# Graph attention weights as a product of two exponentials, in place of start-up transfers in order of use

## The chip, the cores and the metric

The kernel runs on one core of one Trainium2 chip. The metric is the device time of one launch in microseconds. Before the change the median of three runs is 2511.33 us (2510.76 to 2514.62). The profiled execution has a span of 2509.0 us and a mean granted TensorE clock of 0.994.

## The reference, cut to what matters

128 graphs of 64 nodes with 256 features go through four layers, each followed by a residual sum and a layer norm: a gated graph network (five recurrent steps with message weights), a two-layer perceptron with an RMS norm on aggregated features, a hyperbolic map, and graph attention. All is float32. The change touches the last layer and the start. The last layer is:

```python
h = hidden @ W_w.T + W_b                  # hidden: (128, 64, 256)
a1, a2 = a_w[:256], a_w[256:]
e, f = h @ a1, h @ a2                     # one number per node each
logits = e[:, :, None] + f[:, None, :] + a_b[0]
u = mask * exp(logits)                    # mask: the adjacency, (128, 64, 64), 0 or 1
a = u / sum(u, axis=2, keepdims=True)
h_prime = a @ h
x = layernorm(x + h_prime)
```

## The kernel before

Two graphs are put side by side on 128 partitions, with zeros in the off-diagonal quarters of the 128 x 128 adjacency block. Four such blocks (eight graphs) are a group, and there are 16 groups. Up to four neighbouring groups are in work at once: every operation of every group is recorded with its engine, an assumed duration and what it reads and writes, and a planner that runs when the kernel is built merges the groups into one order of instructions for each engine. So a changed operation or assumed duration changes the whole order.

The assumed durations and the model of transfers in the planner (cut):

```python
def op(self, eng, us, run, w=(), r=(), kb=0): ...       # kb: size of a transfer
# in the planner: a transfer has a bus with a speed, and at most eight are under way
DMA = (2.0, 330.0, 1.0)
TRANSFERS = 8
elif o.kb and e != "POOL":
    t = max(t, self.lands[0])
```

The start (cut): weights are loaded raw, turned on TensorE, and multiplied with each other, so that five steps have their own gate weights. Sixteen transposes of the identity into a bank that nobody reads stand ahead of the first useful ones.

```python
for s in range(NF):
    nc.vector.memset(edge[s].tile(), 0.0)
load(0)                                                  # x and adjacency of group 0, SP queue
# ... small vectors on the POOL queue ...
raw_in(w_hh, "ACT", "h", 0, 4)
raw_in(w_ih, "ACT", "A", 0, 4)
raw_in(w_ih, "ACT", "B", 1, 2)
warm = const.tile([P, NB], F32, name="warm")
flow.op("ACT", 1.5, lambda: nc.scalar.activation(warm, one4, AF.Tanh))
ps_x = bank("ps_x")
for i in range(16):
    pe(128, lambda i=i: nc.tensor.transpose(ps_x[...], ident.tile(), ident.tile()), [ps_x], [ident])
raw_in(w_hh, "SP", "h", 1, 2)
wm_in(0)
load(1)
for l in range(1, L):
    wm_in(l)
raw_in(att_w, "SP", "adjT", 0, 2)
# ... later, also on SP: w1s, w2s (1 MB each)
```

The attention of a group (cut). `wattT` holds the turned weights and three more columns: zeros, and the weights times `a1` and `a2`; `wb_r` holds the bias with a one and two numbers more. So one product gives `h`, a column of ones, `e` and `f`:

```python
ho = u("h", "ho", (P, NB, D + 3))
for b in range(NB):
    ps = bank("ps_a")
    for k in range(KD):
        pe(256, ... matmul(ps[:, :D + 3], x3T[:, k, b*P:(b+1)*P], wattT[:, k, :], k, KD), ...)
    dve(256, ... nc.vector.tensor_add(ho[:, b, :], ps[:, :D + 3], wb_r.tile()), ...)
ps_e = bank("ps_e")
for b in range(NB):
    turn(... nc.tensor.transpose(ps_e[:, b*P:(b+1)*P], ho[:, b, D+1:D+2].to_broadcast([P, P]), ident.tile()), ...)
lg = u("U", "lg", (P, NB, N))
for t in range(2):
    dve(256, ... nc.vector.tensor_tensor(lg[q], tiles_of(ps_e.tile())[q, :, q], ho[q, :, D+2] broadcast, OP.add), ...)
act(256, ... nc.scalar.activation(lg.tile(), lg.tile(), AF.Exp, bias=ab_c.tile()), ...)
for t in range(2):
    dve(256, ... nc.vector.tensor_mul(ed[q, :, q], lg[q], adjT[q, :, q]), ...)
for b in range(NB):
    ps = bank("ps_att")
    pe(257, ... matmul(ps[:, :D + 1], ed[:, b, :], ho[:, b, :D + 1], 0, 1), ...)
    dve(4, ... nc.vector.reciprocal(rd[:, b:b+1], ps[:, D:D+1]), ...)
    dve(256, ... scalar_tensor_tensor(y3[:, b, :], ps[:, :D], rd[:, b:b+1], x3[:, b, :], OP.mult, OP.add), ...)
```

Of the kernel before, what the change touches and what calls it, by code (L numbers as in the profile page):

```python
# [42 lines left out]
class Op:  # L43
    __slots__ = ("eng", "us", "run", "stream", "n", "kb", "need", "then", "bufs", "opens", "id", "way")

    def __init__(self, eng, us, run, stream, n, kb):
        self.eng, self.us, self.run, self.stream, self.n, self.kb = eng, us, run, stream, n, kb
        self.need, self.then, self.bufs, self.opens, self.id, self.way = 0, [], (), None, 0, 0.0


class Plan:


    def __init__(self, flow):
        self.flow = flow
        ops = [o for s in flow.streams for o in s]
        self.need = [o.need for o in ops]
        self.at = [0.0] * len(ops)
        self.uses = {}
        self.clock = dict.fromkeys(flow.AHEAD, 0.75)  # L60
        self.queues = [{e: deque(o for o in s if o.eng == e) for e in self.clock} for s in flow.streams]
        self.banks = [0.0] * BANKS
        self.left, self.first, self.bus, self.done = len(ops), 0, 0.0, 0.0
        self.lands = [0.0] * flow.TRANSFERS
        self.past, self.order = None, []

    def copy(self):
        c = Plan.__new__(Plan)
        c.flow, c.need, c.at, c.uses = self.flow, self.need.copy(), self.at.copy(), self.uses.copy()
        c.clock, c.banks, c.lands = self.clock.copy(), self.banks.copy(), self.lands.copy()  # L70
        c.queues = [{e: d.copy() for e, d in q.items()} if self.first <= s < self.first + 2 * self.flow.WINDOW else q
                    for s, q in enumerate(self.queues)]
        c.left, c.first, c.bus, c.done = self.left, self.first, self.bus, self.done
        c.past, c.order = (self.past, self.order), []
        return c

    def advance(self, until, rank):
# [3 lines left out]
        while self.left and clock["PE"] < until:  # L81
            best = None
            for s in range(self.first, min(self.first + flow.WINDOW, len(self.queues))):
                for e, q in self.queues[s].items():
                    opened = False
                    for _, o in zip(range(flow.AHEAD[e]), q):
                        t = max(clock[e], at[o.id])
                        if o.opens is not None:
                            if opened or not banks or need[o.id]:
                                opened = True  # L90
                                continue
                            t = max(t, banks[0])
                        elif need[o.id]:
                            continue
                        elif o.kb and e != "POOL":
                            t = max(t, self.lands[0])
# [20 lines left out]
            if o.kb:  # L117
                self.bus = max(self.bus, end + flow.DMA[0]) + o.kb / flow.DMA[1]
                end = self.bus + flow.DMA[2]
                if o.eng != "POOL":  # L120
                    self.lands = [*self.lands[1:], end]
# [19 lines left out]
class Flow:  # L141
# [13 lines left out]


    DMA = (2.0, 330.0, 1.0)
    TRANSFERS = 8
# [9 lines left out]
    def op(self, eng, us, run, w=(), r=(), kb=0):  # L168
        o = Op(eng, us, run, len(self.streams) - 1, len(self.ops), kb)
# [46 lines left out]
    def issue(self):  # L216
        self.ways()
        ranks = (lambda s, o: (s, o.n), lambda s, o: (s if o.kb else -s, o.n), lambda s, o: (self.LAG * s - o.way, s, o.n))
# [21 lines left out]
def kernel(  # L240
# [73 lines left out]
    def pe(n, run, w, r):  # L314
        flow.op("PE", {512: 0.86, 256: 0.435, 257: 0.44, 128: 0.23}.get(n, 0.3), run, w, r)
# [31 lines left out]
    def load(g):  # L347
        s = g % NF
        xt = unit("B", s, f"x_{g}", (P, NB, D))
        flow.op("SP", 0.5, lambda: nc.sync.dma_start(xt.tile(), x_rows[g]), [xt], kb=512)  # L350
        for t in range(2):
            q = quads[t]
            flow.op("SP", 0.75, lambda q=q, t=t: nc.sync.dma_start(edge[s][q, :, q], adj_blocks[g, t]),
                    [(edge[s], t)], kb=64)
        loads[g] = xt
# [3 lines left out]
    for s in range(NF):  # L359
        nc.vector.memset(edge[s].tile(), 0.0)  # L360
# [32 lines left out]
    wattT = fixed([P, KD, D + 3], "wattT")  # L393
# [9 lines left out]
    for v, n in ((b_ih, NV), (b_hh, NV), (b1, KH), (rms_w, KH)):  # L403
        flow.op("POOL", 0.55, lambda v=v, n=n, at=at: nc.gpsimd.dma_start(
            vecs[at:at + n, :], v.rearrange("(c p) -> c p", p=P)), [(vecs, at)], kb=3)
        at += n
    flow.op("POOL", 0.55, lambda: nc.gpsimd.dma_start(nmr.tile(), nodemask.rearrange("(k t) n -> k (t n)", t=2)),
            [nmr], kb=32)

# [4 lines left out]

    def raw_in(src, eng, tag, i, n):
        q = {"SP": nc.sync, "ACT": nc.scalar}[eng]
        raw = unit(tag, S, f"raw_{src.tensor.name}{i}", (P, n, D), bufs(tag))
        flow.op(eng, 0.6, lambda: q.dma_start(
            raw.tile(), src.rearrange("(c p) d -> p c d", p=P)[:, 4 * i:4 * i + n, :]), [raw], kb=128 * n)
        raw_of[src.tensor.name, i] = raw  # L420

    wms = []

    def wm_in(l):
        wm = unit("UVZRU"[l], S - l // 4, f"wm{l}", (P, KD, D))
        flow.op("SP", 0.6, lambda: nc.sync.dma_start(
            wm.tile(), w_msg[l].rearrange("(k p) e -> p k e", p=P)), [wm], kb=256)
        wms.append(wm)

    raw_in(w_hh, "ACT", "h", 0, 4)  # L430
    raw_in(w_ih, "ACT", "A", 0, 4)
    raw_in(w_ih, "ACT", "B", 1, 2)

    warm = const.tile([P, NB], F32, name="warm")
    flow.op("ACT", 1.5, lambda: nc.scalar.activation(warm, one4, AF.Tanh))
    ps_x = bank("ps_x")
    for i in range(16):
        pe(128, lambda i=i: nc.tensor.transpose(ps_x[:, i % 4 * P:(i % 4 + 1) * P], ident.tile(), ident.tile()), [ps_x], [ident])
    raw_in(w_hh, "SP", "h", 1, 2)
    wm_in(0)  # L440
    load(1)
    for l in range(1, L):
        wm_in(l)
    raw_in(att_w, "SP", "adjT", 0, 2)
# [43 lines left out]
    for l in range(L):  # L488
# [25 lines left out]
        sums("DVE", 0.7) if l == 0 else sums("POOL", 1.32)  # L514

    w1s = fixed([P, KD, H], "w1s")
    flow.op("SP", 0.6, lambda: nc.sync.dma_start(w1s.tile(), w1.rearrange("(k p) h -> p k h", p=P)), [w1s], kb=1024)
    w2s = fixed([P, KH, D], "w2s")
    flow.op("SP", 0.6, lambda: nc.sync.dma_start(w2s.tile(), w2.rearrange("(k p) d -> p k d", p=P)), [w2s], kb=1024)
# [3 lines left out]
    def everywhere(v, n, name, more=0):  # L523
        t = fixed([P, n + more], name)
        flow.op("POOL", 0.55, lambda: nc.gpsimd.dma_start(
            t[:, :n], bass.AP(tensor=v.tensor, offset=v.offset, ap=[[0, P], [1, n]])), [t], kb=n / 2)
        return t
# [3 lines left out]
    wb_r = everywhere(att_b, D, "wb_r", 3)  # L531
# [17 lines left out]
    pool(0.11, lambda: nc.gpsimd.memset(wattT[:, :, D:D + 1], 0.0), [(wattT, D)])  # L549
    pool(0.11, lambda: nc.gpsimd.memset(wb_r[:, D:D + 1], 1.0), [wb_r])  # L550
    for i in range(2):
        for o, k in ((wattT[:, 0, :], 0), (wattT[:, 1, :], 1), (wb_r.tile(), None)):
            src = wb_r if k is None else (wattT, k)
            dve(256, lambda o=o, i=i: nc.vector.scalar_tensor_tensor(
                junk_d.tile(), o[:, :D], 1.0, a_r[:, i * D:(i + 1) * D], OP.mult, OP.mult,
                accum_out=o[:, D + 1 + i:D + 2 + i]), [src if k is None else (wattT, (k, i))], [src, a_r])

    def group(g):
# [217 lines left out]
        flow.op("SP", 0.5, lambda: nc.sync.dma_start(xr.tile(), x_rows[g]), [xr], kb=512)  # L776
# [145 lines left out]
        ho = u("h", "ho", (P, NB, D + 3))  # L922
        for b in range(NB):
            ps = bank("ps_a")
            for k in range(KD):
                pe(256, lambda ps=ps, b=b, k=k: matmul(
                    ps[:, :D + 3], x3T[:, k, b * P:(b + 1) * P], wattT[:, k, :], k, KD), [ps], [(x3T, b // 2), wattT])
            dve(256, lambda ps=ps, b=b: nc.vector.tensor_add(ho[:, b, :], ps[:, :D + 3], wb_r.tile()),  # L928
                [(ho, b)], [ps, wb_r])
        ps_e = bank("ps_e")  # L930
        for b in range(NB):
            turn(lambda b=b: nc.tensor.transpose(
                ps_e[:, b * P:(b + 1) * P], ho[:, b, D + 1:D + 2].to_broadcast([P, P]), ident.tile()), [ps_e], [(ho, b)])
        lg = u("U", "lg", (P, NB, N))
        for t in range(2):
            q = quads[t]
            dve(256, lambda q=q: nc.vector.tensor_tensor(
                lg[q], tiles_of(ps_e.tile())[q, :, q], ho[q, :, D + 2].unsqueeze(2).to_broadcast([N, NB, N]), OP.add),
                [(lg, t)], [ps_e, ho])
        act(256, lambda: nc.scalar.activation(lg.tile(), lg.tile(), AF.Exp, bias=ab_c.tile()), [lg], [lg, ab_c])  # L940

        for t in range(2):
            q = quads[t]
            dve(256, lambda q=q: nc.vector.tensor_mul(ed[q, :, q], lg[q], adjT[q, :, q]), [(ed, t)], [lg, adjT])
        y3 = rows("y", "y3")
        rd = tiny("rd")
        for b in range(NB):
            ps = bank("ps_att")
            pe(257, lambda ps=ps, b=b: matmul(ps[:, :D + 1], ed[:, b, :], ho[:, b, :D + 1], 0, 1),
               [ps], [ed, (ho, b)])  # L950
            dve(4, lambda ps=ps, b=b: nc.vector.reciprocal(rd[:, b:b + 1], ps[:, D:D + 1]), [(rd, b)], [ps])
# [42 lines left out]
```

## Time and profile before

| what | value |
|---|---|
| time, median of 3 | 2511.33 us |
| span of the profile | 2509.0 us |
| TensorE (PE) busy | 2438.9 us, 97% |
| VectorE (DVE) busy | 1659.8 us, 66% |
| ScalarE (ACT) busy | 1188.6 us, 47% |
| GpSimd (POOL) busy | 179.1 us, 7% |
| moved by the queues | 35.12 MB, mean 14 GB/s |

Busy time of an engine is time in which it had an instruction under way. For each group of instructions the profile gives the number, the busy time, the mean duration in ns, and the idle time of the engine just before, with the instruction that ended it. PE runs the matmuls, PEld loads their weights beside them. A float32 matmul stands as two records; a transpose stands as one. SPq, ACTq and POOLq are the queues from which transfers are issued.

### The profile page before, as it was taken

How to read it: one execution, taken by the hardware profiler on the slowest of the kernel's cores; microseconds unless marked ns; L12 is line 12 of the kernel's file. 1: busy time of each engine (PE TensorE's matmuls, PEld its weight loads, DVE VectorE, ACT ScalarE, POOL GpSimd, SP SyncE). 2: the span in 40 equal slices, each digit the busy share in tenths (PEclk: the TensorE clock that was granted, in tenths of full speed). 3: DMA queues.
4: the chain of work that ended last, by engine and by line, in shares of the span. 5: the costliest groups of instructions: out<-in, count | busy, mean ns of one | idle time of the engine just before them, and what ended most of it. 6: DMA issues, size and time to landing. Idle time of an engine off the chain costs nothing. (4 is left out here: it accounts for less than half of the span.)

```text
span 2509.0 us, 31864 instructions
## 1 busy us (share of the span) xinstructions
PE 2438.9 (97%) x11986; PEld 2047.4 (82%) x11986; DVE 1659.8 (66%) x3725; ACT 1188.6 (47%) x2500; POOL 179.1 (7%) x146
## 2 busy tenths in 40 slices
PE   8999999999999999999999999999999999999995
PEld 6887887888787887887878878887888887878874
DVE  2656677667577676666776766676766665666766
ACT  3444445445445445445454454455445445444643
POOL 4001000000001000000010000010000000000011
PEclk9999999999999999999999999999999999999998
DMA  4000000000000000000000000000000000000000
GB/s 125 1 1 9 1 9 20 1 9 28 1 20 9 20 9 20 1 19 9 1 28 1 20 9 1 9 28 1 20 28 1 11 18 1 9 20 9 1 9 26
DMA packets 39146, 35.12 MB, mean 14 GB/s; under 512 B 9892, under 2 KB 38592, under 8 KB 38992
## 3 DMA queue, kind: packets, MB, share of 16 engines
q1 hardware_dynamic: 37264, 31.20, 3.9%
q8 instruction: 95, 1.56, 0.3%
q10 hardware_dynamic: 1328, 1.31, 0.2%
q0 software_dynamic: 400, 0.57, 0.1%
q14 instruction: 59, 0.48, 0.1%
HBM read 24.69 MB, written 8.39 MB: 13 GB/s over the span
## 5 line engine op out<-in xcount | busy, mean ns | idle before, releaser
L609 PE MATMUL p_hn<-hT,w_hn 128*128 128x256 f32 x1280 | 320.7, 380 | 0.0
L609 PE MATMUL p_in<-agg,w_in 128*128 128x256 f32 x1280 | 311.9, 379 | 0.0
L609 PEld LDWEIGHTS p_in<-agg,w_in 128*128 128x128 f32 x1280 | 241.3, 190 | 32.6 <-issue 1.0
L609 PEld LDWEIGHTS p_hn<-hT,w_hn 128*128 128x128 f32 x1280 | 229.0, 191 | 29.4 <-issue 4.8
L312 PE MATMUL ps_o<-w2s,hid 128*128 128x256 f32 x1024 | 234.0, 381 | 3.4 <-DVE n L905 3.0
L312 PE MATMUL ps_hid<-aggm,w1s 128*128 128x512 f32 x512 | 229.0, 592 | 0.0
L312 PEld LDWEIGHTS ps_o<-w2s,hid 128*128 128x128 f32 x1024 | 193.2, 191 | 30.2 <-issue 3.2
L624 POOL TENSOR_TENSOR rstd<-ve,pow 128x4 f32<-128x4 f32 (+1 forms) x64 | 77.5, 1211 | 1823.6 <-DVE ve L622 1823.5
L713 ACT ACTIVATE V<-V,half_b 128x256 f32<-128x256 f32 x160 | 72.8, 500 | 267.9 <-DVE V L709 267.9
L312 PEld LDWEIGHTS ps_hid<-aggm,w1s 128*128 128x128 f32 x512 | 95.3, 190 | 97.1 <-issue 92.4
L609 PE MATMUL p_r<-hT,a 128*128 128x256 f32 x640 | 155.1, 380 | 7.2 <-ACT U L739 5.9
L609 PE MATMUL p_u<-tA,s 128*128 128x256 f32 x640 | 157.3, 384 | 4.9 <-DVE tA L692 2.3
L609 PE MATMUL p_w<-tA,s 128*128 128x256 f32 x640 | 160.2, 380 | 1.7 <-DVE tA L692 1.7
L609 PE MATMUL p_r<-agg,a 128*128 128x256 f32 x640 | 153.4, 380 | 5.9 <-ACT agg L602 4.9
L609 PE MATMUL p_v<-tB,s 128*128 128x256 f32 x640 | 156.7, 379 | 0.0
L678 ACT ACTIVATE hnb<-p_hn,half_b 128x256 f32<-128x256 f32 x320 | 135.5, 471 | 44.6 <-PE p_hn L609 42.4
L609 PE MATMUL p_v<-tB,na 128*128 128x256 f32 x640 | 153.8, 380 | 2.1 <-DVE V L709 2.0
L722 DVE SCALAR_TENSOR_TENSOR R<-R,hnb 128x512 f32<-128x512 f32 x80 | 56.1, 701 | 150.1 <-ACT R L713 150.0
L609 PE MATMUL p_w<-hT,s 128*128 128x256 f32 x640 | 155.4, 379 | 0.0
L602 ACT COPY agg<-ps_agg 128x512 f32<-128x512 f32 x160 | 93.0, 583 | 119.2 <-PE ps_agg L312 94.4
L312 PEld LDWEIGHTS ps_agg<-edge,hr 128*128 128x128 f32 x1024 | 134.6, 191 | 11.3 <-ACT hr L672 4.9
L609 PEld LDWEIGHTS p_r<-hT,a 128*128 128x128 f32 x640 | 120.2, 190 | 28.4 <-ACT U L739 7.9
(206 smaller groups left out, 4447.1 us busy)
## 6 DMA issues: line engine op xcount, KB each, us to landing
x<-in_x_dram SPq DMA_DIRECT2D x16, 512.0 KB, 3.8
xr<-in_x_dram SPq DMA_DIRECT2D x16, 512.0 KB, 3.5
out_dram<-x_n SPq DMA_DIRECT2D x16, 512.0 KB, 2.8
edge<-in_adj_dram SPq DMA_DIRECT2D x32, 64.0 KB, 2.3
wm<-in_L_gnn_weight_dram SPq DMA_DIRECT2D x5, 256.0 KB, 7.3
w1s<-in_L_gnn_W_dram SPq DMA_DIRECT2D x1, 1024.0 KB, 6.8
w2s<-in_L_gnn_W_dram SPq DMA_DIRECT2D x1, 1024.0 KB, 9.6
aw_in_L_gnn_w_hh_dram<-in_L_gnn_w_hh_dram ACTq DMA_DIRECT2D x1, 512.0 KB, 5.3
```

Of the source, the lines that this page charges most:

```text
L312: nc.tensor.matmul(o, lhsT, rhs, start=(k == 0), stop=(k == nk - 1))
L602: act(512, lambda: nc.scalar.copy(dst[:, :, half(n)], blocks_of(ps.tile())), [(dst, n)], [ps])
L609: pe(256, lambda c=c, k=k: nc.tensor.matmul(ps[:, c * HR:(c + 1) * HR], w[:, k, c * P:(c + 1) * P], v(k), start=first and c == k == 0, sto ...
L624: pool(1.1, lambda: nc.gpsimd.tensor_tensor(rstd[:, :m, :], ve[:, :m, :], pow2[:, :m, :], OP.pow), [rstd], [ve])
L678: act(300, lambda c=c: nc.scalar.activation(hnb[:, c, half(n)], p_hn[:, c * HR:(c + 1) * HR], AF.Identity, bias=half_b[:, 2 * KD + c:2 * K ...
L713: act(256, lambda c=c: nc.scalar.activation(o[:, c, :], src(c), AF.Tanh, bias=half_b[:, i * KD + c:i * KD + c + 1], scale=0.5), [(o, c)], ...
L722: dve(512, lambda: nc.vector.scalar_tensor_tensor(t.tile(), t.tile(), 1.0, hnb[:, :, half(n)], OP.add, OP.mult), [t], [t, (hnb, (n, 0)), ( ...
```

## The change

The weight exp(e_i + f_j + a_b) is exp(e_i) times exp(f_j) with the constant shared out. A factor of the row falls out of the quotient (the code still multiplies it in ahead of the reciprocal and out again behind it, in two small products a block). So the sums can use the plain transposed adjacency with features that are scaled by exp(f_j), and no 64 x 64 matrix of weights is made. The bias of the features is added at the end, since the weights of a row sum to one; with it go the reads and writes of the `edge` tile in this layer. What ScalarE does on the way out of PSUM is an exponential of two columns and a copy with that scale.

At the same time the ordering of the start is left out: the planner's model of transfers, the ordered issue, the warming transposes and the early table load are gone, ten transfers are issued from the ACT queue at once, and the three `edge` tiles are zeroed on POOL instead of DVE.

```diff
-    nc.vector.memset(edge[s].tile(), 0.0)
+    flow.op("POOL", 0.5, lambda t=edge[s]: nc.gpsimd.memset(t.tile(), 0.0), [edge[s]])
 ...
-                        elif o.kb and e != "POOL":
-                            t = max(t, self.lands[0])
-        ranks = (..., lambda s, o: (s if o.kb else -s, o.n), ...)
+        ranks = (..., lambda s, o: (-s, o.n), ...)
-        flow.op("SP", 0.5, lambda: nc.sync.dma_start(xt.tile(), x_rows[g]), [xt], kb=512)
+        flow.op("SP", 4.0, lambda: nc.sync.dma_start(xt.tile(), x_rows[g]), [xt])
 ...
-    raw_in(w_hh, "ACT", "h", 0, 4)
-    raw_in(w_ih, "ACT", "A", 0, 4)
-    raw_in(w_ih, "ACT", "B", 1, 2)
-    flow.op("ACT", 1.5, lambda: nc.scalar.activation(warm, one4, AF.Tanh))
-    for i in range(16):  ... transposes of the identity ...
-    raw_in(w_hh, "SP", "h", 1, 2); wm_in(0); load(1); wm_in(1..4); raw_in(att_w, "SP", "adjT", 0, 2)
+    for src, eng, tags in ((w_hh, "SP", ("h", "h")), (w_ih, "ACT", ("A", "B")), (att_w, "ACT", ("adjT",))):
+        ... one transfer for each tag ...
+    for l in range(L):  ... wm on "ACT" ...
+    ... w1s, w2s on "ACT"; load(1) only after the gate weights ...
 ...
+    dve(256, lambda: nc.vector.tensor_add(a_sum.tile(), a_r[:, :D], a_r[:, D:]), [a_sum], [a_r])
+    dot(... cs, wb_r, a_sum ...); cs = (cs + ab_c) / 2
 ... the attention of a group:
-            dve(256, ... nc.vector.tensor_add(ho[:, b, :], ps[:, :D + 3], wb_r.tile()), ...)
-        ps_e, its four transposes, lg (two additions), one Exp of 128 x 256, two products into ed
+            act(4, ... nc.scalar.activation(hw[:, b, D:], ps[:, D:D + 2], AF.Exp, bias=cs.tile()), ...)
+            act(256, ... nc.scalar.activation(hw[:, b, :D], ps[:, :D], AF.Identity, scale=hw[:, b, D:D+1]), ...)
+        dve(1030, ... nc.vector.tensor_add(x3.tile(), x3.tile(), over(wb_r.tile(), NB)), ...)
         for b in range(NB):
-            pe(257, ... matmul(ps[:, :D + 1], ed[:, b, :], ho[:, b, :D + 1], 0, 1), ...)
-            dve(4, ... reciprocal(rd, ps[:, D:D + 1]))
+            pe(256, ... matmul(ps[:, :D + 1], adjT[:, b, :], hw[:, b, :D + 1], 0, 1), ...)
+            dve(4, ... tensor_mul(rd, ps[:, D:D + 1], hw[:, b, D + 1:]))
+            dve(4, ... reciprocal(rd, rd))
+            dve(4, ... tensor_mul(rd, rd, hw[:, b, D + 1:]))
```

## The prediction

> **What bounds the kernel now.** I read the head of the page first, for the engine that has no time left.
>
> ```profile
> span 2509.0 us, 31864 instructions
> PE 2438.9 (97%) x11986; PEld 2047.4 (82%) x11986; DVE 1659.8 (66%) x3725; ACT 1188.6 (47%) x2500; POOL 179.1 (7%) x146
> ...
> PE   8999999999999999999999999999999999999995
> ```
>
> PE is busy in 2438.9 of 2509 us; only its first and its last slices are not full. So a change brings time in four ways only: work taken off PE, PE idle time at the start, in the middle, or at the end. The table of 50 us windows shared out the 70 us of idle time: 7 us in the first 50, about 31 us in the 47 windows between 50 and 2400, never more than 3.7 in one, and the rest, about 32 us, behind 2400. DVE with 66% and ACT with 47% have slack in the middle; what they do matters there only as latency.
>
> The waits of PE, cut to the first 60 us and then to the time behind 2400 us, show what ends the idle time at both ends (total, times, longest):
>
> ```profile
> PE ps_agg L312 <- DVE edge L655: 3.2, 1, 3.2
> PE ps_x L438 <- POOL ident masks.py:199: 2.5, 1, 2.5
> PE ps_wmT L492 <- DMA wm<-in_L_gnn_weight_dram: 1.4, 1, 1.4
> ```
>
> ```profile
> PE ps_T L579 <- DVE x_n L638: 9.7, 1, 9.7
> PE ps_o L312 <- DVE n L905: 3.0, 1, 3.0
> PE ps_e L932 <- DVE ho L928: 2.7, 5, 1.3
> PE ps_att L312 <- DVE edge L944: 2.4, 1, 2.4
> ```
>
> At the end it is DVE, with the chain of the last two groups, and two of the four lines belong to the attention that is changed. Last, the groups of instructions of the old attention, with shapes kept apart (busy us, mean ns):
>
> ```profile
> L928 DVE TENSOR_TENSOR ho<-ps_a,wb_r 128x259 f32<-128x259 f32 x64 | 26.3, 419 | 15.5 <-PE ps_a L312 15.5
> L932 PE MATMUL ps_e<-ident,ho 128*128 128x128 f32 x64 | 14.1, 279 | 3.3 <-DVE ho L928 3.3
> L937 DVE TENSOR_TENSOR lg<-ps_e,ho 64x256 f32<-64x256 f32 x32 | 13.5, 421 | 11.2 <-PE ps_e L932 11.0
> L944 DVE TENSOR_TENSOR edge<-lg,adjT 64x256 f32<-64x256 f32 x32 | 13.4, 417 | 5.5 <-ACT lg L940 5.0
> L940 ACT ACTIVATE lg<-lg,ab_c 128x256 f32<-128x256 f32 x16 | 8.1, 504 | 21.6 <-DVE lg L937 21.5
> ```
>
> The whole old attention apart from its large products is 53 us of DVE, 8 us of ACT and 64 transposes in 2509 us. What is changed is small.
>
> **What the Trainium skill says.** "TensorE: Matmul & The Clock Gate", section "What's actually happening": PE starts at half its clock and is let to the full one only after some 3.4 us of activity; a pause as long throttles it again. The trace agrees: at 16.75 us, behind a pause of 3.2 us, eight records of the aggregation took 2.04 us; at 22.95 us eight of the same took 1.05. "ScalarE: Activation LUTs", section "Table sets: the hidden batching unit": exp and tanh are in one set, so an exponential among tanhs needs no switch. The trace agrees: of the 33 table loads, 1283 ns each, one stands at the line of the Exp, and the changed program has 33 loads too. Same page, "What ACT_TABLE_LOAD costs": a pointer operand adds about 93 ns to an activation. No row here isolates it; I use it for one estimate below. "DMA: Bandwidth & Descriptors", "Queues, rings and completion order": the DMA engines take packets from the queues in turn, so a queue filled early takes bandwidth from one with urgent data. In the first 20 us the trace has the 16 engines 0.95 busy at 296 GB/s, so there is something to take.
>
> **The change part by part.**
>
> *PE work.* The built program has 6492 PE operations where there were 6572: 64 transposes of `ps_e` and 16 warming ones less. A mean of 279 ns is latency; in a row, transposes start every 0.112 us (at 8.41 us nine loads of transposes took 1.01 us). 64 x 0.112 = 7.2 us off the bound engine. One column less of 259 in 128 products is under half a per cent of the 63.6 us of `ps_a`: 0.2 us. The warming ones ran while PE had nothing to do: nothing. Sum: -7.2 us.
>
> *DVE.* Off: 26.3 + 13.5 + 13.4 = 53.2 us. On: one addition of 128x1024 a group. Additions take 0.419 us at 256 (L928) and 0.684 at 512, so 1.035 ns an element; at 1024 that is 0.684 + 512 x 0.001035 = 1.21 us, times 16 = 19.4. And two small products a block of about 0.16 us like the other small DVE rows: 128 x 0.16 = 20.5. Net -13 us of 1660, in slack.
>
> *ACT.* Off: 8.1 us. On, in each of 64 blocks: an Exp of two columns, 0.207 us like the 128x4 Tanh of the map, plus 0.093 for its pointer, 0.30 (an estimate), and an Identity of 256 columns from PSUM, 0.471 like the `hnb` row. 64 x 0.77 = 49, net +41 us, to 1230 us or 49%. In slack as well; a block takes ACT 0.77 us while PE needs 4 records of 0.215, 0.86 us, for the next one. So ACT keeps up.
>
> *Start.* In the trace, PE stood until 16.75 us for an `edge` product on DVE, which had waited in DVE's order behind a bias product for `a_r` (DVE sat idle 4.9 us until 14.59, "DMA a_r"). The new order has the same trap: a sum of the halves of `a_r` stands as DVE's 14th row, ahead of the transposed-adjacency copy, the `edge` products and the weight copies. And `a_r` is issued later, since POOL first zeroes three `edge` tiles. A POOL memset of 128 columns took 0.20 us and one of 1 column 0.10, so about 0.5 for 512, times three = 1.5 us. From 6.89 to 8.4 us, landing 7.7 us after as before, 16.1; then 0.42 for the sum, 0.68 for the copy, 0.60 for the two products: PE goes on at about 17.9, 1.2 us later. What PE has done by then differs more. Before, 42 transposes (x, both weights, adjacency, first message weight, vectors) were behind it; in the new order only 14 stand ahead of the aggregation. 28 x 0.112 = 3.1 us are still to do. Sum +4.3. The order in which the rest of the start stands then keeps PE fed: all five sets of weight products, 5 x 5.2 us, before the first group.
>
> *End.* The old chain from the last `ps_a` (done about 2494.6) to the first `ps_att` (2497.81) is ho, ps_e, lg twice, exp, edge twice: 3.2 us. The new one is 0.30 + 0.47 and two hand-overs, about 1.0: -2.2. Behind it, three small DVE operations instead of one a block: 4 x 2 x 0.16 = +1.3. The addition of the bias to x3 lies beside the 5.3 us of `ps_a`. The group before it saves about 3.4 us of DVE work on that stretch and gets back 2.5: -0.9. In the old order the third-last group's attention stood in the middle of the last two groups' chains (its `ho` delays the norm at 2422 us, its sums at 2440 to 2444); in the new order it stands some 60 rows of PE earlier, while group 15 still fills PE. That was about 2 us on the chain of the end. Sum: -4 us.
>
> *Middle.* The orders are planned anew with other durations, so 31 us of small gaps are drawn again. I see no reason for a sign: 0, with plus or minus 10.
>
> -7.2 + 4.3 - 4 + 0 = -6.9: 2511.3 - 6.9 = about 2504 us.
>
> **The rivals.** *ACT latency takes the place of DVE latency.* Scale and exponential stand in ACT's order behind whatever came before, and `ps_a` banks are held by two activations instead of one addition. The list of waits has PE waiting for ACT 17 us in all between 60 and 2400 (`U`, `agg`, `x3T`, `hr`, `Z`), more than for DVE in each single line; 41 us more ACT work could raise this. If each of the 16 groups loses 1 us, PE's gain is gone twice over: 2520. Against it: ACT is idle half of the time, and PE has other groups' work to take. *The start is worse than I reckon.* 2 MB of perceptron weights go out on ACT's queue at once beside the x and weights that PE needs; if `a_r` or the message weights land 10 us later, the start costs 15 instead of 4: 2515. Against it: all that the start needs from SP's queue is its first 1.4 MB, and both queues together need 20 us at 296 GB/s for everything. *The new plan is simply better*, with the edge tile free after layer 1 and a shorter chain in every group: if half of the gaps in the middle go, 2490. Against it: hardly any of those gaps are waits of the attention (`ps_e` 0.6 us in the middle).
>
> **Range and chances.** The parts' uncertainty is about 2 us for PE's work, 5 for the start, 5 for the end and 10 for the middle, together some 12. I choose 2504 and 2488 to 2521. Two per cent are 50 us, four times that spread, and only a new systematic stall of 3 us a group would reach it: 0.015 faster, 0.965 the same, 0.02 slower.
>
> **What would show it.** PE busy about 7 us lower, near 2432. In PE's waits up to 60 us, `ps_agg` waits for DVE's `edge` until about 18 us and DVE for `a_r`. DVE near 1647, ACT near 1230, 33 table loads. In the end, no line for `ps_e`, PE's idle time behind the same work 4 us less. I am wrong if PE's waits for ACT in the middle double, if PE is idle over 20 us in the first 60, or if PE busy doesn't fall.

## The result and the profile after

| | before | after |
|---|---|---|
| time, median of 4 runs | 2512.97 us (2510.76 to 2514.8) | 2523.07 us (2522.06 to 2524.53) |
| span of the profile | 2509.0 us | 2522.8 us |
| PE busy | 2438.9 us | 2433.8 us |
| PE idle, 0 to 50 us | 7.0 us | 15.5 us |
| PE idle, 50 to 2400 us | 30.9 us | 40.6 us |
| PE idle behind 2400 us | 32.1 us | 33.0 us |

The ratio after to before is 1.0041, 95% interval 1.0024 to 1.0058: the changed kernel takes some 10 us more, where 7 us less were predicted. First the head of the page of the changed kernel:

```profile
span 2522.8 us, 31907 instructions
PE 2433.8 (96%) x11906; PEld 2039.3 (81%) x11906; DVE 1642.8 (65%) x3738; ACT 1229.5 (49%) x2611; POOL 177.8 (7%) x147
...
PE   7999999999999999999999999999999999999995
```

PE still bounds the kernel and has less to do; DVE and ACT fell and rose as they should. So the 13.8 us of span were lost in PE's idle time. The table of windows says where. Its columns are the stretch, its length, busy us and instructions of PE, PEld, DVE, ACT and POOL, granted clock, share of the DMA engines, GB/s. First the kernel before:

```profile
0.00:50.00 50.00, 42.95 (x197) 33.46 (x198) 13.67 (x43) 15.84 (x38) 15.82 (x26) 0.93 0.47 146
50.00:2400.00 2350.00, 2319.11 (x11471) 1956.18 (x11470) 1569.41 (x3420) 1131.43 (x2382) 148.52 (x109) 1.00 0.03 11
2400.00:2509.00 109.00, 76.87 (x320) 57.80 (x319) 76.75 (x263) 41.36 (x81) 14.77 (x12) 0.91 0.06 20
```

And the changed kernel:

```profile
0.00:50.00 50.00, 34.53 (x143) 25.10 (x144) 11.31 (x34) 12.82 (x32) 19.46 (x29) 1.00 0.48 146
50.00:2400.00 2350.00, 2309.42 (x11389) 1944.17 (x11389) 1548.94 (x3445) 1162.54 (x2467) 144.69 (x108) 1.00 0.04 11
2400.00:2522.80 122.80, 89.84 (x378) 70.01 (x376) 82.55 (x261) 54.13 (x113) 13.68 (x11) 0.87 0.04 13
```

Length minus PE busy is the idle time of the table above: 8.4 us more at the start, 9.7 more in the middle, 0.8 more behind 2400. One correction belongs to it: the 16 warming transposes of the kernel before counted as 3.67 us of busy PE (from 2.47 us on) and are gone. So of the 5.1 us that PE busy fell, 3.7 were never work and 1.4 are left, and the start's loss of idle time, with the warming counted as idle, is 15.5 - (7.0 + 3.7) = 4.8 us.

**The start.** The waits of PE in the first 60 us (total, times, longest):

```profile
PE ps_cols L417 <- DMA vecs<-in_L_gnn_rms_weight_dram: 10.7, 1, 10.7
PE ps_agg L300 <- DVE edge L632: 4.7, 1, 4.7
```

PE did nothing for 10.7 us: its first instruction turns a small vector that the POOL queue brought last, and the instructions behind it stay behind it in PE's order, though the x that eight of them turn had landed at 6.01 us. The timeline of the start (start, us, engine, operation, the idle time before it and who ended it):

```profile
9.26 0.55 POOL L496 DMA_DIRECT2D a_r<-in_L_gnn_a_w_dram  x1 [2.16 <-DMA vecs<-in_L_gnn_b_ih_dram]
10.75 0.28 PE L417 MATMUL ps_cols<-ident,vecs 28*128 28x28 f32 x1 [10.75 <-DMA vecs<-in_L_gnn_rms_weight_dram]
...
17.19 0.42 DVE L531 TENSOR_TENSOR a_sum<-a_r 128x256 f32<-128x256 f32 x1 [5.34 <-DMA a_r<-in_L_gnn_a_w_dram]
...
18.14 0.60 DVE L632 TENSOR_SCALAR edge<-edge 64x256 f32<-64x256 f32 x2
18.79 1.22 PE L300 MATMUL ps_agg<-edge,x 128*128 128x128 f32 x4 [4.72 <-DVE edge L632]
...
20.44 1.91 PE L438 MATMUL ps_w<-ident,w_in_L_gnn_w_hh_dram 128*128 128x128 f32 x8
```

The second wait is the trap of the prediction, link by link: `a_r` issued at 9.26, its sum on DVE at 17.19, the `edge` product behind it, PE at 18.79. It is the one that counts. Only 14 instructions stand between the two waits, and the aggregation behind them would have stood until 18.79 if they had been done earlier; so on this reading the first wait cost nothing of its own, though no run takes it away alone.

The last line shows half speed. Behind the two pauses eight transposes take 1.91 us, where eight of the same kind took 1.04 us at 7.64 us of the kernel before. This is what the Trainium skill describes in "TensorE: Matmul & The Clock Gate", section "What's actually happening": behind a pause PE starts at half its clock. The trace agrees with that, though the half speed lasted about 5 us of work (18.79 to 23.7), longer than the 3.4 us of the page, and the column of the granted clock shows 1.00 for this stretch; the durations tell it, not the column. But the kernel before has the same behind its own pause at 16.75 us. With 0.213 us from start to start at half speed and 0.110 at full, the transposes and aggregations behind the second pause lost 2.2 us, and those behind the pause of the kernel before 1.9: a difference of 0.3.

**The middle.** PE's waits from 60 to 2400 us, and the row for all of DVE's waits for the reload `xr`:

```profile
PE ps_hr L566 <- DVE hT L711: 6.8, 10, 1.4
PE p_r L586 <- ACT agg L579: 6.5, 6, 1.4
PE ps_T L556 <- DVE x_n L615: 4.8, 3, 3.1
PE p_u L586 <- DVE tA L669: 4.8, 7, 1.4
PE p_w L586 <- DVE tA L669: 3.8, 2, 3.3
...
DVE y L760 <- DMA xr<-in_x_dram: 7.3, 11, 1.4
```

The first line is to be read with the last. `xr` is a group's x, loaded a second time for the residual of the first layer. DVE adds it in `y`, 64 times; in 11 of the 16 groups the first of these additions stood waiting for the transfer, 0.66 us on average, and everything behind it in DVE's order waited too, `hT` among it, for which PE then waits 6.8 us. Before, that row was two waits:

```profile
DVE y L783 <- DMA xr<-in_x_dram: 1.5, 2, 1.1
```

Why, is seen in the view of the one tile. Its last line is the time from issue to landing (least, median, most), for the kernel before

```profile
  DMA xr<-in_x_dram: 1.5, 2
...
DMA to landing us min/median/max: 3.2/3.5/3.8
```

and for the changed kernel

```profile
  DMA xr<-in_x_dram: 7.3, 11
...
DMA to landing us min/median/max: 3.8/3.9/5.0
```

The old planner counted 0.5 + 2 + 512/330 + 1 = 5.05 us for this reload, the new one counts 4.0. From the issue of `xr` to the group's first addition the timelines show a median of 5.2 us before and 4.05 us after (16 groups each). The 5.2 are a distance with room in it, as the landing took 3.5. The 4.05 are not: with a landing of 3.9 they are little more than the transfer itself. How near the addition really stands shows where nothing waits for the reload, in `after_noxr` below.

**The end.** PE's waits behind 2400 us:

```profile
PE ps_T L556 <- DVE x_n L615: 10.9, 1, 10.9
PE ps_sup L300 <- DVE tan L859: 4.2, 1, 4.2
PE ps_o L300 <- DVE hid L814: 3.4, 1, 3.4
```

The waits for `ps_e` and `ps_att`, 5.1 us, are gone as predicted. The waits for the norm and for `tan` have grown in their place, from 9.7 and 2.0 to 10.9 and 4.2 us.

**The new attention itself** is as it was reckoned (groups of instructions with shapes kept apart: count, busy us, mean ns):

```profile
L909 ACT ACTIVATE hw<-ps_a,hw 128x256 f32<-128x256 f32 x64 | 30.4, 475 | 1.7
L907 ACT ACTIVATE hw<-ps_a,cs 128x2 f32<-128x2 f32 x64 | 16.7, 262 | 11.7 <-PE ps_a L300 9.3
L911 DVE TENSOR_TENSOR x_n<-x_n,wb_r 128x1024 f32<-128x1024 f32 x16 | 19.5, 1217 | 5.7 <-PE ps_T L556 5.6
L917 DVE TENSOR_TENSOR rd<-ps_att,hw 128x1 f32<-128x1 f32 x64 | 9.3, 147 | 26.2 <-PE ps_att L300 26.1
```

Predicted were 471 ns for the copy, 300 for the exponential (an estimate with the Trainium skill's figure for a pointer operand, "ScalarE: Activation LUTs", section "What ACT_TABLE_LOAD costs"; measured 262, so the estimate was high), 1210 for the addition and 160 for the small products.

### The profile page after: what moved, and what is told of

The parts are those of the page before. It is cut to its first block, busy times and chain, and to the rows that moved or that the text cites. A ratio compares the mean times of both kernels' runs of the same rounds, so it can differ in the third digit from the quotient of the medians.

```text
span 2522.8 us, 31907 instructions
## 1 busy us (share of the span) xinstructions
PE 2433.8 (96%) x11906; PEld 2039.3 (81%) x11906; DVE 1642.8 (65%) x3738; ACT 1229.5 (49%) x2611; POOL 177.8 (7%) x147
## 4 chain that ended last, share of the span: by engine, by line
PE 71%; DVE 12%; ACT 4%; POOL 2%; DMA 2%; issue 1%; POOLq 0%; ACTq 0%; DVEq 0%; SPq 0%
PE ps_hid L300 9%; PE ps_o L300 9%; PE p_v L586 8%; PE p_w L586 8%; PE p_in L586 7%; PE p_r L586 7%; PE p_hn L586 7%; PE p_u L586 4%; PE ps_agg L300 4%; PE ps_a L300 2%; POOL rstd L601 2%; DMA xr<-in_x_dram 2%; PE ps_hr L566 2%; DVE st L596 2%; DVE tA L669 1%
## 5 line engine op out<-in xcount | busy, mean ns | idle before, releaser
L300 PEld LDWEIGHTS ps_o<-w2s,hid 128*128 128x128 f32 x1024 | 195.4, 192 | 30.9 <-DVE hid L814 3.8
L794 DVE TENSOR_TENSOR sqs<-sqs,sq 128x512 f32<-128x512 f32 x112 | 77.4, 691 | 121.3 <-ACT sq L791 121.3
L586 PEld LDWEIGHTS p_u<-tA,s 128*128 128x128 f32 x640 | 119.5, 191 | 30.9 <-DVE tA L669 8.0
```

Of the source, the lines that this page charges most:

```text
L300: nc.tensor.matmul(o, lhsT, rhs, start=(k == 0), stop=(k == nk - 1))
L586: pe(256, lambda c=c, k=k: nc.tensor.matmul(ps[:, c * HR:(c + 1) * HR], w[:, k, c * P:(c + 1) * P], v(k), start=first and c == k == 0, sto ...
L794: dve(512, lambda sq=sq: nc.vector.tensor_add(sqs.tile(), sqs.tile(), sq.tile()), [sqs], [sqs, sq])
```

## The experiments

My theory after this reading: the attention brings a few microseconds; the start and the waits for `xr`, both taken to come from the transfers' side of the change, take more than that. Rivals: the activations hold PE up in the new attention; or the planner simply drew a worse order, as it does for any change. All ratios are to the kernel before, on the same chip. "Replanned" means that the order of instructions is made anew, which moves thousands of PE instructions; "same order" means that PE's order of the changed kernel is kept to within a dozen places.

### One half of the change at a time

`newatt_oldstart` is the kernel before, transfers and all, with the new attention; `oldatt_newstart` is the changed kernel with the old attention. Both are replanned.

```diff
  newatt_oldstart: the kernel before, and in the attention of a group
-    ho, ps_e, lg, exp, ed ...
+    hw = exp and scaled copy on ACT; adjT as weights of the sums ...
  oldatt_newstart: the changed kernel, and there the reverse
```

> The kernel before with the new attention alone; its start and its planner's model of transfers stay. Theory A (the loss is the start, 10 us, and the planner's assumption for the residual's reload of x, 10 us in the middle; the attention itself gains 7): about 2505 us, PE idle 7 us in the first 50 and about 31 us between 50 and 2400, DVE waits for xr at most 2 us. Rival B (the activations of the new attention cause the gaps in the middle): about 2515 us, idle in the middle about 40 us. Rival C (each new plan draws its gaps anew): anywhere between 2498 and 2520, with 22 to 45 us in the middle.

> The changed kernel with the old attention put back. A: about 2530 us, 7 more than the changed kernel, idle in the middle about 40 us with some 7 us of DVE waits for xr, idle in the first 50 us about 15. B: about 2520, idle in the middle about 31 us. C: 2515 to 2540, with no rule for the middle.

Measured: 0.9987 (0.998 to 0.9994) and 0.9985 (0.9978 to 0.9992). Each half alone is a little faster than the kernel before, and together they are slower: the halves don't add up. All three expectations for `oldatt_newstart` were too high. In `oldatt_newstart` the start's loss is there (PE idle 14.1 us in the first 50), yet the middle is 2.5 us better than before. Either the halves work on each other, or the plan that a kernel draws is worth as much as what was changed. One execution of `newatt_oldstart`, its profiled one, took 5212 us with PE busy for 5181 us, over twice as long for the same instructions, and is left out; so it was run again:

> The new attention with the start and the planner's model of transfers of before, once more, for a whole profile. If the transfers' side of the change made the loss: PE idle 7 us in the first 50, waits for xr at most 2 us, about 2512 again. In the middle between 27 and 38 us idle, depending on the plan drawn; PE busy about 2434.

0.9987 (0.998 to 0.9994) again, with PE busy 2434.3 us and idle 8.4, 36.5 and 31.4 us in the three stretches.

### The planner's draw

The planner keeps 8 partial plans while it searches. With 12 or 16 the operations stay the same, to the last one, and only their order differs.

```diff
-    WINDOW, STRETCH, WIDTH, LAG = 4, 25.0, 8, 40.0
+    WINDOW, STRETCH, WIDTH, LAG = 4, 25.0, 12, 40.0     # or 16
```

> The changed kernel planned with 12 candidate plans kept at each step instead of 8; no operation and no assumed duration differs. A and B: 2523 within 3 us, waits for xr about 7 us. C: the idle time in the middle moves by 5 us or more in either direction, and the time with it.

> The kernel before, planned with 12 candidates kept instead of 8; no operation and no duration differs. If the draw of the plan alone moves the time (theory C): 3 to 8 us in either direction, with the idle time of the middle; if plans of the same operations are alike: within 2 us of the kernel before, 29 to 33 us idle in the middle.

> The new attention with the old start, another plan of the same operations. Against the first plan of them: 3 to 8 us in either direction if the draw matters, within 2 us if not. The mean of both against the mean of both plans of the kernel before is the attention's own gain: 7 less as predicted, or about 3 as the first plan had it.

> The old attention with the new start, a second plan of the same operations. The first plan took 0.9985 of before although its start is as bad (14 us idle). If that was a lucky draw: 1.001 to 1.005, 5 us or more above the first plan, with over 30 us idle in the middle. If the new start costs nothing when the attention is the old one: 0.998 to 1.000 again.

> The changed kernel in a third plan, 16 candidates kept. If the planner's assumption of 4.0 us for the reload makes the waits for xr whatever the draw: again 5 to 8 us of them where the reload lands in 3.9 us, and 1.001 to 1.004. If they are the draw of two plans: under 2 us.

> The new attention with the old start in a third plan (0.9987 and 0.9958 so far). Spread of the draw alone: 0.995 to 0.999; waits for xr under 2 us, as the planner reckons 5 us for the reload there. If it is under 0.9958 it is the fastest.

Measured, all in one table (ratio to before):

| plans kept | old attention, old start | new attention, old start | old attention, new start | new attention, new start |
|---|---|---|---|---|
| 8 | 1 | 0.9987 | 0.9985 | 1.0041 |
| 12 | 0.9986 | 0.9958 | 1.0058 | 1.0016 |
| 16 | | 0.9961 | | 1.0010 |

The draw is worth up to 0.0073, 18 us, with nothing else changed (third column; intervals 0.9978 to 0.9992 and 1.0043 to 1.0073). So `oldatt_newstart` was a lucky draw and the first experiment by itself proved nothing. Of the 20.3 us between the spans of its two plans 9.9 are idle time of PE, and 10.4 are busy time, 2435.4 and 2445.8 us for the same instructions. PE's waits in the middle of `oldatt_newstart_w12` show of what kind the idle part was:

```profile
PE p_u L580 <- DVE tA L663: 10.7, 10, 2.1
PE p_r L580 <- ACT agg L573: 9.7, 9, 1.6
```

These are hand-overs inside the gated steps (6.7 and 4.7 us in the first plan), not the attention and not `xr` (2.3 us there). What lengthened the busy time no run shows.

Over the draws: with the old start the new attention has a mean of 0.9969 against 0.9993, which is 0.0024 or 6 us in its favour. With the new attention the new start has a mean of 1.0022 against 0.9969, 0.0053 or 13 us against it; with the old attention, 1.0021 against 0.9993, 7 us against it, from two draws that lie 18 us apart. Under the new start no gain of the attention can be told from so few draws. The fastest version of all is `newatt_oldstart_w12`, at 2504.29 us (0.9944 to 0.9973), level with `newatt_oldstart_w16` within the noise and ahead of both kernels:

```profile
span 2502.5 us, 31917 instructions
PE 2433.8 (97%) x11922; PEld 2042.0 (82%) x11922; DVE 1643.4 (66%) x3741; ACT 1228.4 (49%) x2610; POOL 178.1 (7%) x144
```

Its PE is as busy as that of the changed kernel to a tenth of a microsecond, though its 16 warming transposes are in that figure; its span is 20.3 us shorter. All of that is idle time.

### The wait for the second x

First the planner was told a longer time for `xr`:

```diff
-        flow.op("SP", 4.0, lambda: nc.sync.dma_start(xr.tile(), x_rows[g]), [xr])
+        flow.op("SP", 5.5, lambda: nc.sync.dma_start(xr.tile(), x_rows[g]), [xr])
```

> The changed kernel with one number of the planner altered: the reload of x for the residual is assumed to take 5.5 us instead of 4.0. A: DVE waits for xr fall from 7.3 us to under 2, PE idle between 50 and 2400 falls from 41 to 31 to 34 us, 2513 to 2516 us. B: the waits for xr fall, the time stays at 2523 within 3. C: the waits for xr fall, the rest of the gaps is drawn anew, 2515 to 2530.

1.0023 (1.0016 to 1.003). The waits fell from 7.3 to 2.8 us and the span by 4.4 us, but the whole order was planned anew, so this can't be told from a draw: the change of WIDTH to 12 gained 4.7 us of span with 5.7 us of such waits left. Then the same order without the need for the reload. The transfer is still made; the additions read a constant that was loaded long before. This leaves out the residual of the first layer:

```diff
-                    y0[:, b, :], ps[:, j * D:(j + 1) * D], nm[:, blk:blk + 1], xr[:, b, :], OP.mult, OP.add),
+                    y0[:, b, :], ps[:, j * D:(j + 1) * D], nm[:, blk:blk + 1], w2s[:, 0, :], OP.mult, OP.add),
```

> The changed kernel, its plan and durations untouched; the residual of the first layer adds a constant tile instead of the reloaded x, so nothing waits for that transfer (the output is another one). Theory A (DVE's waits for xr make the larger gaps of the middle): PE idle between 50 and 2400 us falls from 41 to 33 to 36, the time by 5 to 8 us against the changed kernel. Rival C (the gaps belong to the plan as drawn, and the xr waits are hidden): the time falls by at most 2 us.

1.0001 (0.9992 to 1.001), so 0.0040 or 10 us below the changed kernel (5 to 15 by the two intervals); the span fell by 8.2 us. The line that stood first in PE's waits in the middle is now

```profile
PE ps_hr L566 <- DVE hT L711: 1.9, 3, 0.7
```

and PE's idle time between 50 and 2400 fell from 40.6 to 34.7 us. Waits of 7.3 us on an engine with a third of its time free cost 8 to 10 us of the whole: DVE's slack was of no use to `hT`, which PE needs at once and which stands behind the waiting addition.

The same run shows how near the addition stands. One reload and its group's first addition, in the changed kernel and then without the need for it:

```profile
1287.41 0.37 SPq L753 DMA_DIRECT2D xr<-in_x_dram  x1
1291.30 0.88 DVE L760 SCALAR_TENSOR_TENSOR y<-ps_hr,nm,xr 128x256 f32<-128x256 f32 x2 [1.04 <-DMA xr<-in_x_dram]
```

```profile
1285.80 0.37 SPq L753 DMA_DIRECT2D xr<-in_x_dram  x1
1288.57 0.87 DVE L760 SCALAR_TENSOR_TENSOR y<-ps_hr,nm,w2s 128x256 f32<-128x256 f32 x2
```

Over the 16 groups the addition comes 2.4 us behind the issue in the median, and in 13 of them sooner than 3.5 us. So this order would have waited for the faster landing of the kernel before as well, only less. All plans together:

| kernels | planner's figure for `xr`, us | landing, median, us | DVE's waits for `xr`, us (times) |
|---|---|---|---|
| old start, either attention, six plans | 5.05 | 3.4 to 3.8 | 0.4 (1) to 1.7 (3) |
| old attention, new start, WIDTH 8, 12 | 4.0 | 3.3, 3.5 | 0.8 (2), 2.3 (4) |
| new attention, new start, WIDTH 8, 12, 16 | 4.0 | 3.9, 3.9, 3.9 | 7.3 (11), 5.7 (10), 4.8 (4) |
| the changed kernel's order, 256 more transposes | 4.0 | 3.5 | 3.5 (5) |
| `after_xr55` | 5.5 | 3.9 | 2.8 (5) |

The figure of 4.0 alone does not make the long waits (second row), nor does the landing of 3.9 alone (last row); the longest stand where both meet.

### The start

The same order with four repairs: the `edge` tiles zeroed on DVE, so that POOL issues its vectors earlier; the sum of `a_r` put off to where it is used; the turning of the small vectors put off behind the gate weights; the perceptron weights on the SP queue.

```diff
-        flow.op("POOL", 0.5, lambda t=edge[s]: nc.gpsimd.memset(t.tile(), 0.0), [edge[s]])
+        flow.op("POOL", 0.5, lambda t=edge[s]: nc.vector.memset(t.tile(), 0.0), [edge[s]])
 ...
-    turn(lambda: nc.tensor.transpose(ps_c[:, :NC], vecs.tile(), ident[:NC, :NC]), [ps_c], [vecs, ident])
+    turn(lambda: None, ...)          # issued behind the last w_hn copy
-    dve(256, lambda: nc.vector.tensor_add(a_sum.tile(), a_r[:, :D], a_r[:, D:]), [a_sum], [a_r])
+    dve(256, lambda: None, ...)      # issued with the product that uses it
-    ... nc.scalar.dma_start(w1s.tile(), ...)     # and w2s
+    ... nc.sync.dma_start(w1s.tile(), ...)       # and w2s
```

> The changed kernel, same plan, with its start mended: edge tiles zeroed on DVE, the sum of the halves of a_r and the turning of the small vectors later in their engines' orders, the two 1 MB weights on SP's queue. Theory A (the start costs 10 us and PE's later work moves forward by what is saved): PE idle in the first 50 us falls from 15.5 to 6 to 9 us, the time by 7 to 10 us. Rival (what is saved at the start is lost again in later waits): the time falls by under 3.

1.0019 (1.001 to 1.0027), 0.0022 or 5.5 us below the changed kernel (1 to 10 by the two intervals), between what theory and rival expected; span 7.6 us less. PE's waits in the first 60 us are now

```profile
PE ps_T L567 <- DMA x<-in_x_dram: 6.1, 1, 6.1
PE ps_adjT L637 <- DMA edge<-in_adj_dram: 2.1, 1, 2.1
PE ps_agg L300 <- DVE edge L643: 1.3, 1, 1.3
```

that is, the data itself: no more waiting for small vectors. The first weight product started at 18.45 us instead of 25.69. PE's idle time in the first 50 us fell by 6.0 us, to 9.5, and PE busy by 1.9 us, with no instruction taken from PE. Of these 1.9, half speed explains about 1.0: the two longest rows of transposes take 1.70 and 1.15 us where they took 1.91 and 1.95. The repair goes further than a return to the old start: the aggregation begins at 12.52 us, where it began at 16.75 in the kernel before, whose idle time with the warming counted as idle was 10.7.

Both repairs at once, again without the residual of the first layer:

```diff
+    after_startfix and after_noxr together
```

> The changed kernel, same plan, with the mended start and the constant tile in place of the reloaded x (the residual of the first layer is left out). If the two losses add: 6 us of the one and 8 to 10 us of the other, so 14 to 16 below the changed kernel, a ratio to before of 0.998 to 0.999, idle 9.5 us in the first 50 and about 36 in the middle. If one hides the other: the better of the two, 1.000 to 1.002.

0.997 (0.9959 to 0.9982), 0.0071 below the changed kernel, where the two repairs by themselves add up to 0.0062. So they are two losses beside each other, and neither hides the other. What remains has the speed of the new attention under the old start, 0.9969 in the mean. But both repairs take away more than the change had added (the kernel before has 1.5 us of waits for `xr` and a slower start than the repaired one), so that this agreement does not prove that nothing else was lost.

### The attention's parts

Is a transpose worth what was reckoned? The same order with 256 needless ones, four ahead of each block's `ps_a`:

```diff
+                if k == 0:
+                    for i in range(4):
+                        nc.tensor.transpose(ps[:, 384:], ident.tile(), ident.tile())
```

> The changed kernel, same plan, with 256 needless transposes (four ahead of each of the 64 blocks' first ps_a product, into columns of the bank that nobody reads), four times the 64 that the change removes. If a transpose costs PE its 0.112 us: 29 us longer, PE busy about 2462, and the 64 were worth 7.2. If the smaller fall of PE's busy time is the truth (1.6 us against the version with the old attention): about 7 us longer.

1.0121 (1.0105 to 1.0136), 0.0080 or 20 us above the changed kernel. PE busy rose from 2433.8 to 2457.1 us, 23.3/256 = 0.091 us each; by the time, 20/256 = 0.078 (14 to 26 us by the two intervals). That is between the two expectations. By these figures the 64 that the change took away were worth 5 to 6 us.

The two small products with which the code multiplies a factor in and out again were left out; as the factor cancels, a plain reciprocal of the sum remains. Once in the same order, once replanned under the old start:

```diff
-            dve(4, ... tensor_mul(rd, ps[:, D:D + 1], hw[:, b, D + 1:]))
-            dve(4, ... reciprocal(rd, rd))
-            dve(4, ... tensor_mul(rd, rd, hw[:, b, D + 1:]))
+            dve(4, ... reciprocal(rd, ps[:, D:D + 1]))
```

> The changed kernel, same plan, without the two small products with exp(e_i) around the reciprocal (128 DVE operations of 0.15 us; the quotient is the same). In slack but for the end: 1 to 2 us less. Rival B (the latency of the new attention's last steps makes gaps in the middle): 4 us less or more, with less idle time between 50 and 2400.

> The new attention with the old start, and the plain reciprocal of the sum without the two small products around it; planned anew. The products are in slack, so 1 to 2 us less than with them, and what the new plan draws: 2505 to 2513 us. If it is below the 2512 of the version with products, it is the fastest so far.

1.0031 (1.002 to 1.0043), against 1.0041 (1.0024 to 1.0058) with them: no difference that can be told, and the span fell by 1.4 us. Replanned: 0.9995 (0.9986 to 1.0004), against 0.9987, 0.9958 and 0.9961 with them, so not better either. DVE's 18.7 us for them are slack.

## Why the prediction was wrong, step by step

The step that failed most is the middle, "I see no reason for a sign: 0". PE's work and the end gave less than reckoned; the start came out nearly as predicted.

- **Middle, "I see no reason for a sign: 0".** PE's idle time rose by 9.7 us there. The waits of DVE for the reload `xr` rose from 1.5 to 7.3 us, and the run without that reload in the same order gave 10 us of time back, 5.9 of them as idle time in this stretch. That the waits cost this much is shown. Where they come from is argued: the diff has a possible reason for a sign, as a reload that had been planned at 5.05 us is planned at 4.0, and the trace of before gave the landing as 3.5 us. Whether 0.5 us of margin would do was never asked. But the addition stood nearer still, 2.4 us behind the issue, and other plans with the same 4.0 had waits of 0.8 and 2.3 us. The part of the 9.7 us that is not `xr` is not explained; new plans of the same operations differ by as much.
- **"Sum: -7.2 us" for PE's work** had the right mechanism; the term "64 x 0.112" was too large. In a row of other work a transpose costs 0.091 us of PE: 5.8 us. With the old start, PE busy was 2439.6 us in the mean of two plans with the old attention and 2434.3 in the mean of three with the new one, 5.3 less; a fourth plan with the new attention (`newatt_oldstart_nomul`) had 2439.8, so this difference by itself shows little. The figure "near 2432" also forgot that the warming transposes are busy time: without them PE busy fell by 1.4 us only. The missing 4 us are busy time of the other instructions, which differs from plan to plan (by 10.4 us in the two plans above).
- **Start, "Sum +4.3".** This was close: 4.8 us more idle time. The trap at `a_r` was right, and PE went on at 18.79 where 17.9 was predicted. The wait of 10.7 us ahead of it was not seen, since "only 14 stand ahead of the aggregation" counted PE's instructions, but not that the first of them waits for POOL's last small vector; as PE had to wait for `a_r` all the same, this did not change the sum. The 28 transposes still to do were put at 0.112 us each, but began at half speed; so did the work behind the pause in the kernel before, and 0.3 us are left of that.
- **End, "Sum: -4 us".** The last chain is shorter, by more than reckoned: from the last group's turning of `x_n` to the end of its last norm it took 17.7 us before (2487.35 to 2505.00) and 14.4 after (2504.25 to 2518.64), 3.3 less, not 0.9. But it took effect only in part. From the aggregation of group 15 to the end it is 87.6 and 86.2 us, 1.4 less, and PE's idle time behind 2400 rose by 0.8. The term "about 2 us" for the third-last group, read from the old order, has no counterpart in the new one: the waits for the norm and for `tan` grew in its place.
- **The rivals.** The latency of ACT: no. PE's waits for it in the middle add up to about 14 us, where they were 17; the largest line is `agg`, which is not in the attention, and a wait of PE for `hw` stands in none of the changed kernel's lists. The worse start: it cost 5 us and not 15 (`a_r` landed about 8 us behind its issue, as before; it was issued 2.4 us later). "The new plan is simply better": the draw is real, and its size, up to 18 us, is above the 10 that I gave the middle. But it was no lucky one here.

The ledger, term by term: PE's busy time without the warming -1.4 (predicted -7.2), start +4.8 (+4.3), middle +9.7 (0), end +0.8 (-4). Together that is the measured +13.8 of span, up to rounding, against the predicted -6.9; by the medians the time rose by 10.

Two things stay open. Why the additions stand so near behind the reload in the changed kernel's plan: the planner's 4.0 us and the landing of 3.9 both have a part, and the one attempt to change the planner's figure alone was replanned. And what makes one plan's gaps, and PE's busy time, larger than another's with `xr` and start alike: I can't name it.

## What to carry to other kernels

When a planner orders in-order engines, its assumed duration of a transfer is a margin, and the margin that the chip leaves can be smaller (here 4.0 us were planned and 2.4 were left). Compare each changed figure with the landing that the trace shows, and ask what stands behind the first reader on its engine; here the slack of that engine didn't protect it. Where an engine waits twice in a row, ask which wait ends last before a cost is put to the first. And before a result of under one per cent is put down to a change, let the planner draw twice or three times with nothing changed, or change one thing in a kept order: here the kept orders settled what the replanned halves could not.

## What the runs showed of the hardware

The same reload of 512 KB lands in 3.3 to 3.5 us (median of an execution) in some kernels and in 3.8 to 3.9 in others. Every kernel with both the new attention and the new start showed 3.9, in every plan, but for the one with 256 more transposes. With the old start it was 3.4 to 3.5, with 3.8 once (`newatt_oldstart_nomul`). The kernel with 256 more transposes, in the changed kernel's own order, had

```profile
DMA to landing us min/median/max: 3.3/3.5/5.0
```

and 3.5 us of waits for `xr` instead of 7.3, in an execution of 2541.28 us, while the other three of that kernel took 2544.46 to 2546.6. So the landing seems to differ between executions; no run shows what sets it.
